# Dense 128x128 blocks for the split operands of the products with adj, and a state shuttle in runs of 32

## The chip, the cores and the metric

The kernel runs on one core of one Trainium2 chip. The metric is device time in microseconds (us) from one launch. Time before: 1607.32 us, the median of three runs (1606.89 to 1607.37).

## The reference, cut to what matters

Thirty-two graphs of 512 nodes with 128 features share one 512x512 matrix `adj`. Four layers follow one another, each a residual around a layer norm and a ReLU. Layer 1 is the one that the change touches: a gated graph network of five steps, whose state `h` is multiplied by `adj` in each of them.

```
h = relu(layernorm(x)); x = x + gcn(h, normalized adj)        # layer 0
h = relu(layernorm(x))                                        # layer 1
for five steps:
    m  = adj @ h
    z  = sigmoid([m, m] @ w3.T + h @ u3.T + b)
    r  = sigmoid([m, m] @ w4.T + h @ u3.T + b)
    hv = tanh([m, m] @ w5.T + (r * h) @ u5.T + b)
    h  = (1 - z) * h + z * hv
x = x + h
h = relu(layernorm(x)); x = x + elu(graph attention(h))       # layer 2
h = relu(layernorm(x)); x = x + graph attention(h)            # layer 3
```

So layer 1 has 32 x 5 = 160 products with `adj`, each of 512x512 by 512x128. Layer 0 has one product for each graph with the normalized matrix (named `an` in the program).

## The kernel before

**Tiles.** A graph's tokens stand in a tile of 128 partitions x 4 chunks (C = 4) x 128 features. In the steps of layer 1 the new state is made with features on the partitions (`hT`), because the gates' products want it so. The next product with `adj` wants it with tokens on the partitions (`h`).

**A product in three (`in_three`, from L604).** A float32 operand is split in a part with its upper bits and a rest, each held in the type fp32r: `cut` (DVE, L613, a bitwise and), `upper` (ACT, L615, a copy of `cut`), `lower` (DVE, L616, `h` less `cut`) and `across` (DVE, L617, formed of `cut` and `h`). `adj` is split in the same way once, at the start (`factors_of`, L417 to L432). TensorE then does twelve products of 128x128 weights with 512 columns (L623): four with `upper`, four with `lower`, then ACT scales the PSUM bank (L630), four with `across`, and ACT copies the bank to `m` (L632). The blocks of `upper`, `lower` and `across` are the weights, which TensorE loads ahead of each product (PEld); the split `adj` is what moves.

**The shuttle (L580 to L589).** In most steps the state is turned from features to tokens not by TensorE but by a DVE transpose of 32x32 blocks into `sq` (L584), four DMAs of 64 KB to DRAM (`far`) and one DMA of 256 KB back into `h`. Its argument `inner` says how `sq` is laid out inside a row of 128 elements: `"(c j)"` leaves runs of 32 elements, `"(j c)"` interleaves the four chunks, so that one chunk's elements lie 16 bytes apart. The shuttle of the steps passes `"(j c)"`. Such an `h` is marked `turned`, and `rows` then picks chunk c of the weights out of it with a step of four elements:

```python
def rows(t, c):
    return t.rearrange("p k (j c) -> p c (k j)", c=C)[:, c] if turned else t[:, c, :]
```

After the last step the same layout is read by the residual (L766). The first state of a graph, the layer norm's `y` of the attention layers (which keeps `"(c j)"`) and the first products of a graph are not `turned`. `shuttle_first` (L591) brings the first state the other way.

**The order.** `Plan` writes the order of all engines' instructions out when the program is built. Each piece of work is given to `op(engine, cost, due, emit, r, w, delay)`: its cost in us, a due time, what it reads and what it writes. A list scheduler plays the engines through with those costs, takes buffers from named pools (`"cut"`: 2, `"upper"`: 2, `"lower"`: 2, `"across"`: 3, `"sq"`: 2, eight PSUM banks), and issues the pieces in the order that comes out. The costs are thus no times of the chip; they set the order alone. `MR` is the cost of one product of L623, `V` that of a float32 DVE operation of 128x512, `A` that of an ACT operation of that size. On the chip each engine runs its own list in order and waits on semaphores. From a model time of 1342 on, the scheduler also fills gaps of TensorE with transposes into a free bank (L321).

**Gates and the rest.** `step` has five products of 128x128 by 128x512 in plain float32 (L729, L730, L736, L743, L744; two instructions each), the tanh operations (L732, L738, L746), and the DVE operations L734, L748, L749, L751. `gat` has the attention: L818, the DVE scores L859 and the mix L885 (L871 for the last four graphs).

Of the kernel before, what the change touches and what calls it, by code (L numbers as in the profile page):

```python
# [10 lines left out]
F32 = mybir.dt.float32  # L11
# [4 lines left out]
ALU = mybir.AluOpType  # L16
# [253 lines left out]
def gnn_stack(ctx: ExitStack, tc: tile.TileContext, a: dict, out: bass.AP):  # L270
# [50 lines left out]
        IDLE_FROM, lambda v: nc.tensor.transpose(v.t[:, 0, :], ident.t, ident.t))  # L321
    op = plan.op
    MM, MM1, TURN, MR = 0.858, 0.224, 0.111, 0.216
    V, A = 0.61, 0.585

    def fixed(shape, name, parts=1, dtype=F32):
        v = Val(None, parts)
# [67 lines left out]
    for c in range(C):  # L395
        p = Val("bank")
        turned.append(p)

        def turn_adj(c=c, p=p):
            for m in range(C):  # L400
                nc.tensor.transpose(p.t[:, m, :], adj_sb.t[:, c, m * P:(m + 1) * P], ident.t)
        op("PE", C * TURN, -800, turn_adj, r=[adj_sb[c], ident], w=[p])
        op("ACT", A, -800, lambda c=c, p=p: nc.scalar.copy(adjT.t[:, :, c * P:(c + 1) * P], p.t), r=[p], w=[adjT[c]])
        if c % 2 == 0:
            junk = Val("r")
            op("ACT", 0.7, -801, lambda c=c, junk=junk: nc.scalar.activation(
                flat(junk.t), adj_sb.t[:, c, :], AF.Copy, accum_out=deg.t[:, c:c + 1]), r=[adj_sb[c]], w=[junk, deg[c]])
# [9 lines left out]
    def factors_of(mT, name, due):  # L417


        upper, lower, across = [fixed([P, C, N], name + k, C, dtype=F32R) for k in ("1", "2", "3")]  # L420
        for c in range(C):
            cut = Val("cut")
            op("DVE", 0.35, due, lambda c=c, cut=cut: nc.vector.tensor_scalar(
                flat(cut.t).bitcast(I32), mT.t[:, c, :].bitcast(I32), UPPER, None, op0=ALU.bitwise_and), r=[mT], w=[cut])
            op("ACT", A, due, lambda c=c, cut=cut: nc.scalar.copy(upper.t[:, c, :], flat(cut.t)), r=[cut], w=[upper[c]])
            op("DVE", V, due, lambda c=c, cut=cut: nc.vector.tensor_sub(
                lower.t[:, c, :], mT.t[:, c, :], flat(cut.t)), r=[mT, cut], w=[lower[c]])
            op("ACT", A, due, lambda c=c: nc.scalar.mul(
                lower.t[:, c, :], lower.t[:, c, :].bitcast(F32), SPLIT), w=[lower[c]])
            op("DVE", V, due, lambda c=c, cut=cut: nc.vector.tensor_sub(  # L430
                across.t[:, c, :], lower.t[:, c, :].bitcast(F32), flat(cut.t)), r=[lower[c], cut], w=[across[c]])
        return upper, lower, across  # L432
    of_adj = factors_of(adjT, "adj", -3.6)

# [61 lines left out]
    def norm_stats(b, due):  # L496
        xb, st, mv, ve = xs[b], Val("st", C), Val("mv"), Val("ve")
        for c in range(C):
            op("DVE", 0.21, due, lambda c=c: nc.vector.bn_stats(st.t[:, c, :], xb.t[:, c, :]), r=[xb[c]], w=[st[c]])

        def aggr():
            for c in range(C):
                nc.vector.bn_aggr(mv.t[:, c, :], st.t[:, c, :])
            nc.vector.tensor_scalar_add(ve.t, mv.t[:, :, 1], EPS)  # L504
        op("DVE", 0.45, due, aggr, r=[st], w=[mv, ve])
        return mv, ve

    def norm_relu(b, y, due, times=None):
# [68 lines left out]
        op("PE", C * TURN, due, turns, r=[y, ident], w=[p, *then])  # L577
        return p

    def shuttle(src, squares, dst, due, soon, inner="(c j)"):  # L580


        sq, far = Val("sq"), Val("far", Q)
        op("DVE", 0.61, soon, lambda: nc.vector.transpose(  # L584
            sq.t.rearrange(f"p q {inner} -> p q c j", c=C), flat(src.t).rearrange(squares, c=C, q=Q)), r=[src], w=[sq])
        for k in range(Q):
            op("SP", 0.44, due, lambda k=k: nc.sync.dma_start(
                far.t[:, :, k, :].rearrange("q i f -> i q f"), sq.t[k * W:(k + 1) * W]), r=[sq], w=[far[k]], delay=4)
        op("SP", 0.4, due, lambda: nc.sync.dma_start(dst.t, far.t.rearrange("q i k f -> (q i) k f")), r=[far], w=[dst], delay=5)  # L589

    def shuttle_first(h, hT, due, soon):  # L591

        sq, far = Val("sq"), Val("far", Q)
        op("DVE", 0.61, soon, lambda: nc.vector.transpose(
            sq.t.rearrange("p k (c i) -> p k c i", c=C), h.t.rearrange("p c (k j) -> p k c j", k=Q)), r=[h], w=[sq])
        for q in range(Q):
            op("SP", 0.44, due, lambda q=q: nc.sync.dma_start(
                far.t[:, :, q, :].rearrange("k j f -> j k f"), sq.t[q * W:(q + 1) * W]), r=[sq], w=[far[q]], delay=4)
        for q in range(Q):
            op("SP", 0.4, due, lambda q=q: nc.sync.dma_start(  # L600
                hT.t.rearrange("p c (q i) -> q p c i", q=Q)[q], far.t.rearrange("k j q (c i) -> q (k j) c i", c=C)[q]),
               r=[far[q]], w=[hT[q]], delay=5)

    def in_three(h, turned, factors, due):  # L604

        cut, upper, lower, across = Val("cut"), Val("upper"), Val("lower"), Val("across")
        upper_of, lower_of, across_of = factors

        def rows(t, c):
            return t.rearrange("p k (j c) -> p c (k j)", c=C)[:, c] if turned else t[:, c, :]
        op("DVE", 0.35, due - 5, lambda: nc.vector.tensor_scalar(  # L613
            flat(cut.t).bitcast(I32), flat(h.t).bitcast(I32), UPPER, None, op0=ALU.bitwise_and), r=[h], w=[cut])
        op("ACT", A, due - 5, lambda: nc.scalar.copy(flat(upper.t), flat(cut.t)), r=[cut], w=[upper])  # L615
        op("DVE", V, due - 5, lambda: nc.vector.tensor_sub(flat(lower.t), flat(h.t), flat(cut.t)), r=[h, cut], w=[lower])  # L616
        op("DVE", V, due - 5, lambda: nc.vector.scalar_tensor_tensor(  # L617
            flat(across.t), flat(cut.t), 1 + 1 / SPLIT, flat(h.t), op0=ALU.mult, op1=ALU.subtract), r=[h, cut], w=[across])
        p, m = Val("bank"), Val("m")

        def times(left, right, first):
            for c in range(C):
                nc.tensor.matmul(flat(p.t), rows(left.t, c), right.t[:, c, :], start=first and c == 0, stop=c == C - 1,  # L623
                                 skip_group_check=True)

        def first_two():
            times(upper, upper_of, True)
            times(lower, lower_of, False)
        op("PE", 8 * MR, due, first_two, r=[upper, lower, upper_of, lower_of], w=[p])
        op("ACT", A, due - 6, lambda: nc.scalar.mul(flat(p.t), flat(p.t), 1 + 1 / SPLIT), w=[p])  # L630
        op("PE", 4 * MR, due, lambda: times(across, across_of, False), r=[across, across_of], w=[p, m])
        op("ACT", A, due - 6, lambda: nc.scalar.copy(flat(m.t), flat(p.t)), r=[p], w=[m])  # L632
        return m

    def product(h, due):

        p, m = Val("bank"), Val("m")
        for c in range(C):
# [5 lines left out]
                        nc.tensor.matmul(flat(p.t)[:, lo * P:hi * P], h.t[:, c, :], right, start=c == lo == 0,  # L644
                                         stop=c == C - 1, skip_group_check=True)
            op("PE", MM, due, times, r=[h[c], adjT, diag[c]], w=[p, m])
        op("ACT", A, due, lambda: nc.scalar.copy(flat(m.t), flat(p.t)), r=[p], w=[m])
        return m

    def normalized(begun):  # L650
# [56 lines left out]
    def ggnn(b, due):  # L707
# [4 lines left out]
        if FAR0 <= b < B - FAR1:  # L712
            shuttle_first(h, hT, due - 2.5, due - 3)
        else:
            p = to_features(h, due - 2, hT)
            op("ACT", A, due - 2, lambda hT=hT: nc.scalar.copy(flat(hT.t), flat(p.t)), r=[p], w=[hT])
        turned = False
        for s in range(STEPS):
            now = due + LANES * s
# [5 lines left out]
    def step(b, s, m, hT, due, lane):  # L725
# [30 lines left out]
        if not EARLY <= due < STEPS * B:  # L756
            p = to_features(new, due + 2, *([] if last else [h]))
            if last:
                op("DVE", V, due + 2, lambda: nc.vector.tensor_add(flat(xs[b].t), flat(xs[b].t), flat(p.t)),
                   r=[p, lane], w=[xs[b]])  # L760
            else:
                op("ACT", A, due + 1, lambda: nc.scalar.copy(flat(h.t), flat(p.t)), r=[p], w=[h])
            return h, False, new
        shuttle(new, "p (c q i) -> p q c i", h, due, due - 5, "(j c)")
        if last:
            op("DVE", V, due + 2, lambda: nc.vector.tensor_add(  # L766
                xs[b].t.rearrange("p c (k j) -> p k c j", k=Q), xs[b].t.rearrange("p c (k j) -> p k c j", k=Q),
                h.t.rearrange("p k (j c) -> p k c j", c=C)), r=[h, lane], w=[xs[b]])
        return h, True, new


# [25 lines left out]
    def gat(b, l, due):  # L797
# [4 lines left out]
        if near:  # L802
            rstd, g = center_relu(b, y, due), Val("off", 2)
            pT = to_features(y, due + 1, gT)
            op("ACT", A, due + 1, lambda: nc.scalar.copy(flat(gT.t), flat(pT.t)), r=[pT], w=[gT])
        else:
            norm_relu(b, y, due)
            shuttle(y, "p (c q j) -> p q c j", gT, due + 0.5, due)
# [47 lines left out]
            op("SP", 0.4, due + 1.5, lambda: nc.sync.dma_start(  # L856
                row.t, line.t.rearrange("c q i -> (c q i)").unsqueeze(0).to_broadcast([P, N])), r=[line], w=[row, e], delay=7)
        for j in range(C):
            op("DVE", 0.68, due + 3, lambda j=j: nc.vector.scalar_tensor_tensor(  # L859
                e.t[:, j, :], matrix(row), h.t[:, j, D + 1:D + 2], mask.t[:, j, :], op0=ALU.max, op1=ALU.mult),  # L860
               r=[row, h[2 + j // 2], mask], w=[e[j]])

# [112 lines left out]
```

## Time and profile before

| | |
|---|---|
| median of three runs | 1607.32 us |
| the profiled execution's own time | 1608.62 us |
| its span, first to last instruction | 1606.8 us |
| TensorE products (PE) | 1589.5 us busy, 6966 instructions |
| TensorE weight loads (PEld) | 1160.8 us busy |
| DVE | 1481.0 us busy, 3751 instructions |
| ACT | 905.6 us busy |
| POOL | 152.5 us busy |
| DMA | 157.66 MB, mean 98 GB/s |
| granted TensorE clock | 1.0 |

An engine's busy time is the union of its records, so records that overlap count once. A record of a product or of a DVE operation is longer than the step from one start to the next, since neighbours overlap. "By shape" below is the table of groups of instructions kept apart by operand shapes: line, engine, operation, output and input names, shapes and count, then busy us, mean ns of one, idle us of the engine just before them. The chain is the work that ended last, followed back from the end; in order of time its rows have a start, a length in us, the line and a count.

### The profile page before, as it was taken

What the parts mean: (1) busy time and instruction counts of PE and PEld (TensorE: products, weight loads), DVE (VectorE), ACT (ScalarE), POOL (GpSimd) and SP (SyncE); (2) the same over time, 40 slices, a digit from 0 to 9 for tenths busy, and PEclk for the clock granted to TensorE, in tenths of its full rate; (3) what the DMA queues carried; (4) which work ended last, traced back from release to release, by engine and by line L of the source; (5) the groups of instructions that cost most, each with busy time, mean ns of one, the idle gap of its engine ahead of it and who ended that gap; (6) DMA issues with size and microseconds to landing.
All of it is one profiled execution on the core that took longest, in us unless ns stands there. A gap on an engine that the chain in (4) does not pass through costs nothing.

```text
span 1606.8 us, 23090 instructions
## 1 busy us (share of the span) xinstructions
PE 1589.5 (99%) x6966; PEld 1160.8 (72%) x6966; DVE 1481.0 (92%) x3751; ACT 905.6 (56%) x1822; POOL 152.5 (9%) x137
## 2 busy tenths in 40 slices
PE   8899999999999999999999999999999999999998
PEld 7576667776777776777777686777676766767678
DVE  8989789999999999999999999999999899987888
ACT  6765555555555545645555645655655555555464
POOL 2111000000100101010110110101010000000010
PEclk9999999999999999999999999999999999999999
DMA  3134233444543443444433534444344424432201
GB/s 105 33 86 110 64 95 97 116 115 113 126 103 101 105 119 92 109 114 120 117 100 93 125 102 122 109 102 112 87 124 116 110 71 106 115 100 66 53 27 41
DMA packets 270141, 157.66 MB, mean 98 GB/s; under 512 B 81248, under 2 KB 236224, under 8 KB 270016
## 3 DMA queue, kind: packets, MB, share of 16 engines
q1 hardware_dynamic: 269728, 155.66, 38.0%
q8 instruction: 55, 0.90, 0.2%
q14 instruction: 70, 0.57, 0.1%
q10 hardware_dynamic: 288, 0.52, 0.1%
HBM read 86.25 MB, written 69.84 MB: 97 GB/s over the span
## 4 chain that ended last, share of the span: by engine, by line
PE 90%; DVE 7%; ACT 1%; issue 1%; POOL 0%; DMA 0%; DVEq 0%; ACTq 0%; POOLq 0%
PE bank L623 32%; PE bank L885 11%; PE bank L729 8%; PE bank L730 8%; PE bank L743 8%; PE bank L744 8%; PE bank L736 8%; PE bank L818 3%; PE bank L693 2%; PE bank L871 1%; DVE sq L584 1%; DVE e L859 1%; PE bank L576 0%; DVE hT L751 0%; DVE hv L748 0%
## 5 line engine op out<-in xcount | busy, mean ns | idle before, releaser
L512 POOL TENSOR_TENSOR rstd<-ve,mhalf 128x4 f32<-128x4 f32 x119 | 140.8, 1184 | 1366.1 <-DVE ve L504 1161.8
L885 PEld LDWEIGHTS bank<-h_gat,e 128*128 128x128 f32 x1792 | 210.5, 191 | 17.9 <-issue 14.4
L623 PE MATMUL bank<-adj,across 128*128 128x512 f32 x640 | 215.3, 462 | 1.6 <-ACT bank L630 1.6
L630 ACT ACTIVATE bank<-bank 128x512 f32<-128x512 f32 x188 | 109.3, 581 | 186.2 <-PE bank L623 183.6
L885 PE MATMUL bank<-h_gat,e 128*128 128x129 f32 x1792 | 212.2, 275 | 0.3 <-DVE v L890 0.3
L623 PE MATMUL bank<-adj,upper 128*128 128x512 f32 x640 | 201.2, 436 | 1.3 <-ACT upper L615 1.3
L623 PEld LDWEIGHTS bank<-adj,across 128*128 128x128 f32 x640 | 156.2, 280 | 41.6 <-issue 22.4
L732 ACT ACTIVATE r<-bank,gate_bw 128x512 f32<-128x512 f32 x160 | 109.7, 686 | 127.3 <-PE bank L730 118.4
L623 PE MATMUL bank<-adj,lower 128*128 128x512 f32 x640 | 177.0, 398 | 0.0
L623 PEld LDWEIGHTS bank<-adj,upper 128*128 128x128 f32 x640 | 154.4, 280 | 30.1 <-issue 8.8
L729 PE MATMUL bank<-m,wT 128*128 128x512 f32 x320 | 164.4, 595 | 3.0 <-ACT m L632 2.5
L736 PE MATMUL bank<-m,wT 128*128 128x512 f32 x320 | 163.4, 594 | 1.8 <-ACT r L732 1.8
L743 PE MATMUL bank<-m,wT 128*128 128x512 f32 x320 | 163.8, 593 | 0.7 <-DVE h_gat L836 0.6
L744 PE MATMUL bank<-rh,wT 128*128 128x512 f32 x320 | 163.5, 592 | 0.7 <-DVE rh L734 0.7
L584 DVE STREAM_TRANSPOSE sq<-hT 128x512 f32<-128x512 f32 x148 | 163.6, 1105 | 0.2
L730 PE MATMUL bank<-hT,wT 128*128 128x512 f32 x320 | 163.4, 592 | 0.0
L746 ACT ACTIVATE hv<-bank,gate_bw 128x512 f32<-128x512 f32 x160 | 109.5, 684 | 93.9 <-PE bank L744 93.0
L623 PEld LDWEIGHTS bank<-adj,lower 128*128 128x128 f32 x640 | 152.9, 280 | 7.2
L859 DVE SCALAR_TENSOR_TENSOR e<-row,h_gat,maskT 128x512 f32<-128x512 f32 x224 | 156.4, 740 | 0.0
L748 DVE TENSOR_TENSOR hv<-hv,hT 128x512 f32<-128x512 f32 x160 | 109.6, 686 | 42.4 <-ACT hv L746 41.9
L615 ACT CAST upper<-cut 128x512 fp32r<-128x512 f32 x188 | 115.2, 613 | 45.7 <-DVE cut L613 44.3
L632 ACT COPY m<-bank 128x512 f32<-128x512 f32 x188 | 109.9, 586 | 53.8 <-PE bank L623 53.3
(155 smaller groups left out, 2504.5 us busy)
## 6 DMA issues: line engine op xcount, KB each, us to landing
far<-sq SPq DMA_DIRECT2D x928, 64.0 KB
h<-far SPq DMA_DIRECT2D x148, 256.0 KB
gT<-far SPq DMA_DIRECT2D x56, 256.0 KB
row<-line SPq DMA_DIRECT2D x56, 256.0 KB
hT<-far SPq DMA_DIRECT2D x112, 64.0 KB
x<-in_x_dram SPq DMA_DIRECT2D x24, 256.0 KB
out_dram<-x SPq DMA_DIRECT2D x20, 256.0 KB
adjT<-in_x_dram SPq DMA_DIRECT2D x8, 256.0 KB
```

Of the source, the lines that this page charges most:

```text
L512: op("POOL", 1.0, due, lambda: nc.gpsimd.tensor_tensor(rstd.t, ve.t, mhalf.t, ALU.pow), r=[ve, mhalf], w=[rstd])
L584: op("DVE", 0.61, soon, lambda: nc.vector.transpose(sq.t.rearrange(f"p q {inner} -> p q c j", c=C), flat(src.t).rearrange(squares, c=C, q= ...
L615: op("ACT", A, due - 5, lambda: nc.scalar.copy(flat(upper.t), flat(cut.t)), r=[cut], w=[upper])
L623: nc.tensor.matmul(flat(p.t), rows(left.t, c), right.t[:, c, :], start=first and c == 0, stop=c == C - 1, skip_group_check=True)
L632: op("ACT", A, due - 6, lambda: nc.scalar.copy(flat(m.t), flat(p.t)), r=[p], w=[m])
L729: nc.tensor.matmul(flat(gate.t), gates.t[:, 0, :], flat(m.t), start=True, stop=False)
L730: nc.tensor.matmul(flat(gate.t), gates.t[:, 1, :], flat(hT.t), start=False, stop=True)
L736: op("PE", MM, due + 0.3, lambda: nc.tensor.matmul(flat(gate.t), gates.t[:, 2, :], flat(m.t), start=False, stop=True, skip_group_check=Tru ...
L743: nc.tensor.matmul(flat(cand.t), gates.t[:, 3, :], flat(m.t), start=True, stop=False)
L744: nc.tensor.matmul(flat(cand.t), u5T.t[:, 0, :], flat(rh.t), start=False, stop=True)
L859: op("DVE", 0.68, due + 3, lambda j=j: nc.vector.scalar_tensor_tensor(e.t[:, j, :], matrix(row), h.t[:, j, D + 1:D + 2], mask.t[:, j, :], ...
L885: nc.tensor.matmul(pt()[:, c, :D + 1], e.t[:, j, i * P:(i + 1) * P], h.t[:, j, :D + 1], start=(j == 0), stop=(j == C - 1))
```

## The change

The shuttle of the steps goes back to `"(c j)"`, the only layout left. `in_three` no longer picks weights with a step of four elements. Instead, where the state comes from a shuttle, `upper` (ACT) and `lower` (DVE) read it in a permuted order in runs of 32 elements and write four dense blocks. `across` is now made of `lower` and `upper` in place of `cut` and `h`, dense on both sides, and so waits for both. In `factors_of` the order of the third factor and the scaling is swapped, and the factor SPLIT sits on the other operand. The rest is costs handed to the scheduler: `V` 0.61 to 0.595, `A` 0.585 to 0.575, a new `COPY` of 0.495 for plain ACT copies and scalings, and smaller values at `cut`, `bn_stats`, the aggregate, the transposes and L859. The same instructions are issued, and no DMA changes in number, size or runs.

```diff
-    V, A = 0.61, 0.585
+    V, A, COPY = 0.595, 0.575, 0.495
...
-            op("ACT", A, due, lambda c=c: nc.scalar.mul(
+            op("DVE", V, due, lambda c=c, cut=cut: nc.vector.scalar_tensor_tensor(
+                across.t[:, c, :], flat(cut.t), -1 / SPLIT, lower.t[:, c, :].bitcast(F32), op0=ALU.mult, op1=ALU.add),
+               r=[lower[c], cut], w=[across[c]])
+            op("ACT", COPY, due, lambda c=c: nc.scalar.mul(
                 lower.t[:, c, :], lower.t[:, c, :].bitcast(F32), SPLIT), w=[lower[c]])
-            op("DVE", V, due, lambda c=c, cut=cut: nc.vector.tensor_sub(
-                across.t[:, c, :], lower.t[:, c, :].bitcast(F32), flat(cut.t)), r=[lower[c], cut], w=[across[c]])
...
-    def shuttle(src, squares, dst, due, soon, inner="(c j)"):
+    def shuttle(src, squares, dst, due, soon):
...
-        op("DVE", 0.61, soon, lambda: nc.vector.transpose(
-            sq.t.rearrange(f"p q {inner} -> p q c j", c=C), flat(src.t).rearrange(squares, c=C, q=Q)), r=[src], w=[sq])
+        op("DVE", 0.617, soon, lambda: nc.vector.transpose(
+            sq.t.rearrange("p q (c j) -> p q c j", c=C), flat(src.t).rearrange(squares, c=C, q=Q)), r=[src], w=[sq])
...
-        def rows(t, c):
-            return t.rearrange("p k (j c) -> p c (k j)", c=C)[:, c] if turned else t[:, c, :]
-        op("DVE", 0.35, due - 5, lambda: nc.vector.tensor_scalar(
+        if turned:
+            def given(t):
+                return t.rearrange("p k (c j) -> p c k j", c=C)
+
+            def made(t):
+                return t.rearrange("p c (k j) -> p c k j", k=Q)
+        else:
+            given = made = flat
+        op("DVE", 0.325, due - 5, lambda: nc.vector.tensor_scalar(
             flat(cut.t).bitcast(I32), flat(h.t).bitcast(I32), UPPER, None, op0=ALU.bitwise_and), r=[h], w=[cut])
-        op("ACT", A, due - 5, lambda: nc.scalar.copy(flat(upper.t), flat(cut.t)), r=[cut], w=[upper])
-        op("DVE", V, due - 5, lambda: nc.vector.tensor_sub(flat(lower.t), flat(h.t), flat(cut.t)), r=[h, cut], w=[lower])
+        op("ACT", COPY, due - 5, lambda: nc.scalar.copy(made(upper.t), given(cut.t)), r=[cut], w=[upper])
+        op("DVE", V, due - 5, lambda: nc.vector.tensor_sub(made(lower.t), given(h.t), given(cut.t)), r=[h, cut], w=[lower])
         op("DVE", V, due - 5, lambda: nc.vector.scalar_tensor_tensor(
-            flat(across.t), flat(cut.t), 1 + 1 / SPLIT, flat(h.t), op0=ALU.mult, op1=ALU.subtract), r=[h, cut], w=[across])
+            flat(across.t), flat(lower.t).bitcast(F32), -SPLIT, flat(upper.t).bitcast(F32), op0=ALU.mult, op1=ALU.add),
+           r=[lower, upper], w=[across])
...
-                nc.tensor.matmul(flat(p.t), rows(left.t, c), right.t[:, c, :], start=first and c == 0, stop=c == C - 1,
+                nc.tensor.matmul(flat(p.t), left.t[:, c, :], right.t[:, c, :], start=first and c == 0, stop=c == C - 1,
...
-        shuttle(new, "p (c q i) -> p q c i", h, due, due - 5, "(j c)")
+        shuttle(new, "p (c q i) -> p q c i", h, due, due - 5)
...
-                h.t.rearrange("p k (j c) -> p k c j", c=C)), r=[h, lane], w=[xs[b]])
+                h.t.rearrange("p k (c j) -> p k c j", c=C)), r=[h, lane], w=[xs[b]])
```

More of the change, by code (lines that the diff above doesn't have):

```diff
@@ L402, in gnn_stack @@
         op("PE", C * TURN, -800, turn_adj, r=[adj_sb[c], ident], w=[p])
-        op("ACT", A, -800, lambda c=c, p=p: nc.scalar.copy(adjT.t[:, :, c * P:(c + 1) * P], p.t), r=[p], w=[adjT[c]])
+        op("ACT", COPY, -800, lambda c=c, p=p: nc.scalar.copy(adjT.t[:, :, c * P:(c + 1) * P], p.t), r=[p], w=[adjT[c]])
         if c % 2 == 0:
@@ L422, in factors_of @@
             cut = Val("cut")
-            op("DVE", 0.35, due, lambda c=c, cut=cut: nc.vector.tensor_scalar(
+            op("DVE", 0.325, due, lambda c=c, cut=cut: nc.vector.tensor_scalar(
                 flat(cut.t).bitcast(I32), mT.t[:, c, :].bitcast(I32), UPPER, None, op0=ALU.bitwise_and), r=[mT], w=[cut])
-            op("ACT", A, due, lambda c=c, cut=cut: nc.scalar.copy(upper.t[:, c, :], flat(cut.t)), r=[cut], w=[upper[c]])
+            op("ACT", COPY, due, lambda c=c, cut=cut: nc.scalar.copy(upper.t[:, c, :], flat(cut.t)), r=[cut], w=[upper[c]])
             op("DVE", V, due, lambda c=c, cut=cut: nc.vector.tensor_sub(
                 lower.t[:, c, :], mT.t[:, c, :], flat(cut.t)), r=[mT, cut], w=[lower[c]])
-            op("ACT", A, due, lambda c=c: nc.scalar.mul(
+            op("DVE", V, due, lambda c=c, cut=cut: nc.vector.scalar_tensor_tensor(
+                across.t[:, c, :], flat(cut.t), -1 / SPLIT, lower.t[:, c, :].bitcast(F32), op0=ALU.mult, op1=ALU.add),
+               r=[lower[c], cut], w=[across[c]])
+            op("ACT", COPY, due, lambda c=c: nc.scalar.mul(
                 lower.t[:, c, :], lower.t[:, c, :].bitcast(F32), SPLIT), w=[lower[c]])
-            op("DVE", V, due, lambda c=c, cut=cut: nc.vector.tensor_sub(
-                across.t[:, c, :], lower.t[:, c, :].bitcast(F32), flat(cut.t)), r=[lower[c], cut], w=[across[c]])
         return upper, lower, across
@@ L498, in norm_stats @@
         for c in range(C):
-            op("DVE", 0.21, due, lambda c=c: nc.vector.bn_stats(st.t[:, c, :], xb.t[:, c, :]), r=[xb[c]], w=[st[c]])
+            op("DVE", 0.192, due, lambda c=c: nc.vector.bn_stats(st.t[:, c, :], xb.t[:, c, :]), r=[xb[c]], w=[st[c]])
         def aggr():
@@ L504, in aggr @@
             nc.vector.tensor_scalar_add(ve.t, mv.t[:, :, 1], EPS)
-        op("DVE", 0.45, due, aggr, r=[st], w=[mv, ve])
+        op("DVE", 0.33, due, aggr, r=[st], w=[mv, ve])
         return mv, ve
@@ L593, in shuttle_first @@
         sq, far = Val("sq"), Val("far", Q)
-        op("DVE", 0.61, soon, lambda: nc.vector.transpose(
+        op("DVE", 0.617, soon, lambda: nc.vector.transpose(
             sq.t.rearrange("p k (c i) -> p k c i", c=C), h.t.rearrange("p c (k j) -> p k c j", k=Q)), r=[h], w=[sq])
@@ L629, in in_three @@
         op("PE", 8 * MR, due, first_two, r=[upper, lower, upper_of, lower_of], w=[p])
-        op("ACT", A, due - 6, lambda: nc.scalar.mul(flat(p.t), flat(p.t), 1 + 1 / SPLIT), w=[p])
+        op("ACT", COPY, due - 6, lambda: nc.scalar.mul(flat(p.t), flat(p.t), 1 + 1 / SPLIT), w=[p])
         op("PE", 4 * MR, due, lambda: times(across, across_of, False), r=[across, across_of], w=[p, m])
-        op("ACT", A, due - 6, lambda: nc.scalar.copy(flat(m.t), flat(p.t)), r=[p], w=[m])
+        op("ACT", COPY, due - 6, lambda: nc.scalar.copy(flat(m.t), flat(p.t)), r=[p], w=[m])
         return m
@@ L646, in product @@
             op("PE", MM, due, times, r=[h[c], adjT, diag[c]], w=[p, m])
-        op("ACT", A, due, lambda: nc.scalar.copy(flat(m.t), flat(p.t)), r=[p], w=[m])
+        op("ACT", COPY, due, lambda: nc.scalar.copy(flat(m.t), flat(p.t)), r=[p], w=[m])
         return m
@@ L715, in ggnn @@
             p = to_features(h, due - 2, hT)
-            op("ACT", A, due - 2, lambda hT=hT: nc.scalar.copy(flat(hT.t), flat(p.t)), r=[p], w=[hT])
+            op("ACT", COPY, due - 2, lambda hT=hT: nc.scalar.copy(flat(hT.t), flat(p.t)), r=[p], w=[hT])
         turned = False
@@ L761, in step @@
             else:
-                op("ACT", A, due + 1, lambda: nc.scalar.copy(flat(h.t), flat(p.t)), r=[p], w=[h])
+                op("ACT", COPY, due + 1, lambda: nc.scalar.copy(flat(h.t), flat(p.t)), r=[p], w=[h])
             return h, False, new
-        shuttle(new, "p (c q i) -> p q c i", h, due, due - 5, "(j c)")
+        shuttle(new, "p (c q i) -> p q c i", h, due, due - 5)
         if last:
@@ L804, in gat @@
             pT = to_features(y, due + 1, gT)
-            op("ACT", A, due + 1, lambda: nc.scalar.copy(flat(gT.t), flat(pT.t)), r=[pT], w=[gT])
+            op("ACT", COPY, due + 1, lambda: nc.scalar.copy(flat(gT.t), flat(pT.t)), r=[pT], w=[gT])
         else:
@@ L858, in gat @@
         for j in range(C):
-            op("DVE", 0.68, due + 3, lambda j=j: nc.vector.scalar_tensor_tensor(
+            op("DVE", 0.65, due + 3, lambda j=j: nc.vector.scalar_tensor_tensor(
                 e.t[:, j, :], matrix(row), h.t[:, j, D + 1:D + 2], mask.t[:, j, :], op0=ALU.max, op1=ALU.mult),
```

## The prediction

> **What bounds the kernel now.** First the page's busy times, then the same by stretches of 100 us.
>
> ```profile
> PE 1589.5 (99%) x6966; PEld 1160.8 (72%) x6966; DVE 1481.0 (92%) x3751; ACT 905.6 (56%) x1822; POOL 152.5 (9%) x137
> ```
>
> ```profile
> 0.00:100.00 100.00, 91.04 (x396) 64.96 (x397) 87.67 (x302) 71.62 (x148) 19.47 (x24) 1.00 0.28 69
> ...
> 900.00:1000.00 100.00, 100.00 (x438) 73.04 (x437) 96.51 (x239) 55.53 (x114) 9.24 (x8) 1.00 0.45 115
> ```
>
> The columns of the second fence are PE, PEld, DVE, ACT and POOL busy. TensorE never rests between 100 and 1500 us: the stretches there lack 3.2 us together, the first 100 us lack 9.0 (chains of latency while the first graphs start), and the end about 5. DVE is second at 92%, and up to 96.5% in mid-run. So time can go in two ways only: TensorE's own steps get shorter, or the few waits around them go. A full PE says nothing on what a product costs, since records overlap; the step from one end to the next does. That is read from the chain of waits in order of time, whose rows here are L623 back to back, and from the weight loads' own line.
>
> ```profile
> L623 PEld LDWEIGHTS bank<-adj,lower x640: 187/310/313, 33.6 to 1541.4; 128*128 128x128 f32 x160
> L623 PEld LDWEIGHTS bank<-an,lower x112: 187/188/191, 62.9 to 1246.9; 128*128 128x128 f32 x112
> ```
>
> ```profile
> 76.96 7.47 PE bank L623 x32
> ```
>
> ```profile
> 174.65 2.84 PE bank L623 x12
> ```
>
> ```profile
> 807.19 1.90 PE bank L623 x8
> ...
> 811.66 0.89 PE bank L693 x8
> 812.56 2.02 PE bank L623 x8
> ```
>
> The first two rows give shortest/median/longest ns of a weight load. There are two kinds and nothing between: about 188 ns (dense: all of `an`, and `adj` where the state is not `turned`) and about 310 ns (the step of four). The trace has 1440 of the latter, 120 products of twelve. Yet a load of 310 ns does not make a product of 310 ns: the 32 products at 76.96 us, all dense, take 7.47/32 = 233 ns each, the twelve strided ones at 174.65 us 2.84/12 = 237 ns. The third fence shows where the stride does bite: eight strided products behind a long float32 product (L730) take 1.90 us, but behind L693, whose products last 0.89/8 = 0.11 us, 2.02 us. A load of 310 ns doesn't fit beside 110 ns of work, so 0.12 us stick out, once per such place.
>
> Last, DVE by shape:
>
> ```profile
> L584 DVE STREAM_TRANSPOSE sq<-hT 128x512 f32<-128x512 f32 x148 | 163.6, 1105 | 0.2
> L584 DVE STREAM_TRANSPOSE sq<-y 128x512 f32<-128x512 f32 x56 | 39.4, 704 | 5.7 <-ACT y L518 5.6
> L594 DVE STREAM_TRANSPOSE sq<-h 128x512 f32<-128x512 f32 x28 | 19.7, 703 | 0.0
> L766 DVE TENSOR_TENSOR x<-x,h 128x512 f32<-128x512 f32 x20 | 21.8, 1091 | 0.0
> ```
>
> The same transpose takes 1105 ns where it writes with a step of 16 bytes (`hT`) and 704 ns in runs of 32 (`y`, `h`); the addition L766, which reads `h` in that step, takes 1091 ns where other additions of the size take some 685 ns.
>
> **What the Trainium skill says.** "SBUF — State Buffer", Specifications (TRN2): lines of 16 bytes, at least two hits in a line for full bandwidth. A step of four fp32 hits each line once. The trace agrees for DVE (+401 ns on the transpose, +406 on the addition) and for the weight load (+122 ns), and runs of 32 show no penalty. "TensorE: Matmul & The Clock Gate", Step-by-step: the next weights load while the present product streams; the trace agrees, 310 ns of load inside a step of 237. "Perfetto Trace Analysis", Identifying the Most-Contended Engine: matmul busy time is a poor measure, weight-load busy a better one. Here the 72% of weight loads would promise much; the steps on the chain say 4 ns, and I go by those. The first-named TensorE page, Architectural detail: ACT and DVE take instructions strictly in order. That matters for the new wait below.
>
> **The change part by part.**
>
> *Weights dense (TensorE, on the path).* (a) 1440 products at 237 instead of 233 to 234 ns: 3.7 ns each, 5.3 us. (b) Groups that follow a short product: the trace has 35 strided groups behind L693 (12), L818 (16) and L885 (7), 0.12 us each: 4.2 us. (c) 107 groups behind L730 or L744 start about 10 ns later than dense ones: 1 us. Sum 10.5 us, all of it steps of an engine without rest. Nothing hides it, and no other engine has to follow faster than it can (next part).
>
> *Transposes and residual (DVE, beside TensorE).* 148 transposes by 0.40 us are 59 us, 28 additions at L766 by 0.41 are 11 us: DVE falls from 1481 to about 1411 us. Worth directly nothing, because TensorE runs over it. Its use is slack: waits of TensorE in mid-run that DVE causes (L836, L890, L895, or ACT behind DVE) can shrink. They are part of the 3.2 us; I take 2 us.
>
> *`upper` and `lower` read permuted.* No row shows ACT or DVE reading a subtraction or a copy in exactly this way. From below: no gain is possible, as the element counts are the same, so +0. From above: the 16-byte step's +0.41 us, on 120 of `lower` (49 us on DVE) and 120 of `upper` (49 us on ACT, which has 1606.8 - 905.6 = 701 us free). I take +0, because the transposes L584 (`y`) and L594 read runs of 32 and cost 704 ns, 20 above a flat operation. Even at the upper end DVE stands at 1460 us, below today.
>
> *`across` from `lower` and `upper`.* The operation stays one DVE operation of 684 ns with two SBUF inputs. New is that it waits for ACT's L615. Behind it on DVE, in order, stand the other lanes' L734, L748 to L751, L859 and the norms; ACT and then TensorE wait for these. From below: 0, where the order puts it after `upper`. From above: if the order stayed as it is, the starts of L617 and ends of L615, paired in order, have `upper` late in 23 of 188 cases, by 39 us together. I take 10 us of DVE time and 0 of TensorE, covered by the 70 us just freed. `across` itself is needed only after eight products and L630. `cut` and `h` come free one operation earlier, `upper` no later, since L623 still reads it last.
>
> *`factors_of`.* One 0.6 us DVE operation goes ahead of ACT's scaling for each of eight blocks. For `adj` the last scaling ends at 26.0 us and the first L623 starts at 32.8; for `an` the last operation ends at 45.6 and the first use is at 62.1. Zero, hidden by these 7 and 16 us.
>
> *The order.* The costs change, so every engine's list is dealt anew. The new ones lie nearer to what this trace shows from start to start: L630 494 ns against `COPY` 0.495, L859 656 against 0.65, `bn_stats` 193 against 0.192, while 0.61 for the `hT` transpose was far from its 0.94 to 1.0 us. That speaks for no more waits than now; bounds -3 and +12 us, taken as part of the 2 us above.
>
> *DMA.* Four stores of 64 KB and a load of 256 KB per shuttle, unchanged in runs of 128 elements; they start up to 0.4 us sooner on SP's queue, at a DMA share of 38%. Zero.
>
> Sum on the profiled execution: 1606.8 - 10.5 - 2 = 1594.3 us of span; its own time lies 1.8 above (1608.62 - 1606.8): 1596.1. The median of the runs lies 1.3 below that execution: 1594.8, so 1595.
>
> **The rivals.**
>
> *More than that (0.07).* The freed DVE also ends the waits at the start and the tail. For: 70 us of slack. Against: the first 100 us wait on chains through ACT, and the tail has no shuttles. All of mid-run and half of the rest: 1606.8 - 10.5 - 3 - 7, about 1587.
>
> *Given back by the order (0.11).* Same mechanism, but the re-dealt lists cost 6 us or so of new waits: 1600 to 1604. For: TensorE has lists of 6966 products with no slack anywhere.
>
> *The loads were never in the way (0.07).* The 4 ns and the 0.12 us are other traffic, or the dense loads keep their wait: 1604 to 1609. Against: the two kinds of groups stand side by side in the same stretches.
>
> *Slower: DVE blocked behind ACT (0.05).* Each L617 parks DVE until L615 is done. DVE has 123 us idle now and 70 more after, so 193 us over 188 products: from a mean wait of 1.0 us on, DVE is the bound. To lose 3 us against now it must also eat TensorE's gain of 12, another 15 us: 1.1 us. At 1.2 us DVE needs 1411 + 226 - the waits that fall in its idle time (at most some 10): 1627 us. Against: 39 us in all even in the old order.
>
> **How the numbers follow.** My case has 0.70. The range 1587 to 1604 takes in the gain of all waits and the order giving back most; some 13 in 100 lie above and 5 below. 0.2% (3.2 us) is about what a measurement of this kernel can tell from no change. Faster by more: my case, the first rival and nearly all of the second, 0.87. Within: 0.07. Slower: 0.06.
>
> **What would show it.** Weight loads of L623 all near 188 ns with PEld busy down by 1440 x 0.122 = 176 us, to about 985; L584 from `hT` near 704 and L766 near 685; DVE busy 1400 to 1425; twelve L623 in 2.80 us; `lower` at 683 to 700; PE still at 99%. Wrong would be: L617 with idle time before it ended by L615 in the tens of us and PE below 98%; `lower` near 1090; or no drop in the steps of L623.

## The result, and the profile after

The changed kernel takes 1588.34 us (median of four runs, 1587.70 to 1589.26) against 1607.34: a ratio of 0.9881, with a 95% interval of 0.9864 to 0.9898. That is 19.0 us saved, where 12 were forecast. The profiled execution has a span of 1586.1 us (1606.8 before) and a time of 1587.88.

First the page's busy times of the kernel after, then the stretch from 900 to 1000 us (columns: PE, PEld, DVE, ACT and POOL busy):

```profile
PE 1573.8 (99%) x6966; PEld 1077.6 (68%) x6966; DVE 1424.2 (90%) x3751; ACT 902.6 (57%) x1822; POOL 153.0 (10%) x137
```

```profile
900.00:1000.00 100.00, 100.00 (x440) 68.39 (x439) 94.11 (x264) 58.16 (x116) 12.59 (x11) 1.00 0.42 106
```

TensorE is as full as it was, and DVE has lost 57 us. The weight loads and the DVE operations by line and by shape (the product of three is now L631, the transpose L585, the residual L774):

```profile
L631 PEld LDWEIGHTS bank<-adj,lower x640: 187/188/189, 32.8 to 1524.8; 128*128 128x128 f32 x160
```

```profile
L624 DVE SCALAR_TENSOR_TENSOR across<-lower,upper 128x512 fp32r<-128x512 f32 x188 | 127.1, 678 | 3.9 <-PE bank L631 2.4 <-ACT upper L622 0.6
...
L623 DVE TENSOR_TENSOR lower<-h,cut 128x512 fp32r<-128x512 f32 x160 | 108.3, 678 | 3.2 <-PE bank L631 2.1
L585 DVE STREAM_TRANSPOSE sq<-hT 128x512 f32<-128x512 f32 x148 | 103.4, 699 | 0.2
...
L774 DVE TENSOR_TENSOR x<-x,h 128x512 f32<-128x512 f32 x20 | 13.5, 675 | 0.0
```

Every load of L631 now takes 186 to 192 ns; the second kind is gone. The transpose fell from 1105 to 699 ns, the residual from 1091 to 675. `lower`, read in runs of 32, costs 678 ns, no more than the flat one did, and ACT's `upper` stayed at 613. The new wait is in the last column of L624: DVE stood idle 0.6 us in all for ACT's `upper`. There is a second new wait, which the prediction did not have: since `across` now reads `upper`, the profile has ACT idle 10.4 us ahead of `upper` (14 times) until an L624 was done. ACT's idle time ahead of `upper` still fell from 45.7 to 33.1 us in all.

The chain of waits in order of time (start us, length us, line, count; L826 is the L818 of before):

```profile
783.27 0.89 PE bank L826 x8
784.16 0.93 PE bank L631 x4
...
789.38 2.79 PE bank L631 x12
```

Twelve products take 2.79 us, 233 ns each, and four of them right behind L826's short products take 0.93 us: nothing sticks out any more.

**Where the 20.7 us of span went.** Records of TensorE overlap (a product of L631 has a record of 395 ns and a step of 233), so a wait shorter than the overlap of some 160 ns leaves no gap. I therefore took each product's step, from the end of the one before to its own end, less 233 ns for the product of three, 429 for half a gate product, 112 for the 128-wide ones. What was over is summed in us: in the column "stride" what strided products took more than dense ones, and by stretch of time all the rest:

| profiled execution | stride | first 60 us | middle | last 150 us |
|---|---|---|---|---|
| before | 10.0 | 14.2 | 8.3 | 3.7 |
| after | 0 | 9.7 | 1.5 | 4.2 |

So 10.0 us are the strided loads, 4.5 lie in the start, 6.8 in the middle, and the tail gives 0.5 back: 20.8. What shortened the start was not taken apart.

### The profile page after: what moved, and what is told of

Read it like the earlier page. It is cut to its first block, busy times and chain, and to the rows that moved or that the text cites. A ratio compares the mean times of both kernels' runs of the same rounds, so it can differ in the third digit from the quotient of the medians.

```text
span 1586.1 us, 23092 instructions
## 1 busy us (share of the span) xinstructions
PE 1573.8 (99%) x6966; PEld 1077.6 (68%) x6966; DVE 1424.2 (90%) x3751; ACT 902.6 (57%) x1822; POOL 153.0 (10%) x137
## 4 chain that ended last, share of the span: by engine, by line
PE 93%; DVE 5%; ACT 1%; issue 0%; POOL 0%; DMA 0%; DVEq 0%; POOLq 0%; ACTq 0%
PE bank L631 32%; PE bank L893 12%; PE bank L737 9%; PE bank L744 9%; PE bank L751 8%; PE bank L752 8%; PE bank L738 8%; PE bank L826 3%; PE bank L701 2%; DVE e L867 1%; PE bank L879 1%; DVE st L554 0%; DVE st L500 0%; PE bank L577 0%; POOL rstd L513 0%
## 5 line engine op out<-in xcount | busy, mean ns | idle before, releaser
L631 PE MATMUL bank<-adj,across 128*128 128x512 f32 x640 | 209.6, 453 | 0.0
L631 PE MATMUL bank<-adj,upper 128*128 128x512 f32 x640 | 200.4, 435 | 0.0
L631 PE MATMUL bank<-adj,lower 128*128 128x512 f32 x640 | 175.1, 395 | 0.0
L744 PE MATMUL bank<-m,wT 128*128 128x512 f32 x320 | 163.3, 594 | 1.8 <-ACT r L740 1.8
L631 PEld LDWEIGHTS bank<-adj,across 128*128 128x128 f32 x640 | 118.0, 189 | 59.6 <-issue 39.2
L631 PEld LDWEIGHTS bank<-adj,upper 128*128 128x128 f32 x640 | 118.8, 188 | 53.2 <-issue 22.6
L746 ACT ACTIVATE z<-bank,gate_bw 128x512 f32<-128x512 f32 x160 | 109.8, 686 | 73.5 <-PE bank L744 69.4
L631 PEld LDWEIGHTS bank<-adj,lower 128*128 128x128 f32 x640 | 120.2, 188 | 28.8
L622 ACT CAST upper<-cut 128x512 fp32r<-128x512 f32 x188 | 114.9, 613 | 33.1 <-DVE cut L620 17.8
```

The lines of the kernel that those rows point to most:

```text
L622: op("ACT", COPY, due - 5, lambda: nc.scalar.copy(made(upper.t), given(cut.t)), r=[cut], w=[upper])
L631: nc.tensor.matmul(flat(p.t), left.t[:, c, :], right.t[:, c, :], start=first and c == 0, stop=c == C - 1, skip_group_check=True)
L744: op("PE", MM, due + 0.3, lambda: nc.tensor.matmul(flat(gate.t), gates.t[:, 2, :], flat(m.t), start=False, stop=True, skip_group_check=Tru ...
L746: op("ACT", A, due - 5, lambda: nc.scalar.activation(flat(z.t), flat(gate.t), AF.Tanh, bias=gate_b["w3"].t, scale=0.5), r=[gate, gate_b["w ...
```

## The experiments

Two theories on what stands beside the strided loads. One: DVE's relief takes waits away from TensorE. Two: the new costs give a better order, whatever the layout. A third showed itself on the way: it also counts whether the lists were made with DVE's load in the costs. All times are medians; the kernel before ran beside them at 1607.0 to 1607.7 us.

| run | layout of the state and weights | costs | us | ratio to before, 95% |
|---|---|---|---|---|
| after | runs of 32, dense | new | 1588.3 | 0.9881 (0.9864 to 0.9898) |
| step of four alone | runs, weights strided | new | 1599.2 | 0.9949 (0.9936 to 0.9961) |
| more DVE work | runs, dense, DVE loaded | new | 1616.8 | 1.0055 (1.0042 to 1.0068) |
| old layout | as before | new | 1613.3 | 1.0037 (1.0024 to 1.0049) |
| old costs | runs, dense | old | 1593.2 | 0.9911 (0.9898 to 0.9925) |
| before, new costs | as before | new | 1621.2 | 1.0091 (1.0076 to 1.0105) |
| more DVE work, priced | runs, dense, DVE loaded | new, and that work | 1602.2 | 0.9966 (0.9953 to 0.9979) |
| before, priced | as before | new, and the slow DVE work | 1600.9 | 0.9966 (0.9953 to 0.9979) |

**The step of four alone.** Same lists in the same order as after.

```diff
+        given = made = flat
+        def rows(t, c):
+            return t.rearrange("p k (j c) -> p c (k j)", c=C)[:, c] if turned else t[:, c, :]
...
-                nc.tensor.matmul(flat(p.t), left.t[:, c, :], ...
+                nc.tensor.matmul(flat(p.t), rows(left.t, c), ...
```

> The changed kernel with the weights of the products with adj picked with a step of four elements again, while the shuttle keeps its runs of 32 and all DVE and ACT operations stay flat and quick; every engine has the same list in the same order as in the changed kernel. The weights picked so are those of other tokens, so this leaves the right pairing of tokens out. My theory (strided weight loads cost TensorE some 10.5 us in steps of L623 and behind short products): 1588.3 + 10.5 = about 1599 us, steps of twelve products back at 2.84 us. Rival (the loads were never in the way, all is order and DVE): 1588 to 1590 us.

Measured 1599.24 us, 10.9 above the changed kernel (give or take 3.4 from the two intervals). The loads and the chain of this run (L627 is the product of three, L822 the L826 of after):

```profile
L627 PEld LDWEIGHTS bank<-adj,lower x640: 187/310/313, 33.9 to 1536.0; 128*128 128x128 f32 x160
```

```profile
789.00 0.89 PE bank L822 x8
789.89 1.05 PE bank L627 x4
...
795.23 2.83 PE bank L627 x12
```

Loads of 310 ns are back, twelve products take 2.83 us, and four behind the short L822 1.05 instead of 0.93: the two terms of the prediction, side by side. The rival that the loads were never in the way is out.

**More DVE work.** Also after's order, with the weights dense.

```diff
+    def more_dve():
+        nc.vector.tensor_sub(idle_dve, idle_dve, idle_dve)   # 128x328
...
+            more_dve()      # ahead of each transpose of the state, and of each L774
```

> The changed kernel with one more DVE subtraction of 328 elements (about 0.40 us) ahead of each of the 148 transposes of the state and each of the 28 residual additions L774, in the same piece of work, so that DVE is loaded and late as before while the weights stay dense and the order of all lists stays. If the 8 us beyond the strided loads come from DVE's relief: 1593 to 1596 us, DVE busy near 1495. If they come from the new order: at most 1590 us. If TensorE's bound hides DVE wholly: 1588 us.

Measured 1616.76 us: 28.4 slower than after and slower than before, far beyond all three expectations. The dose was a little high: the added subtraction takes 0.41 us from start to start, 72 us for 176 of them, and DVE is busy 1488 us against 1481 in the kernel before. The stretch from 100 to 1450 us of this run, then of the kernels after and before:

```profile
100.00:1450.00 1350.00, 1335.83 (x5617) 886.31 (x5616) 1252.33 (x3201) 744.21 (x1455) 117.93 (x100) 1.00 0.41 106
```

```profile
100.00:1450.00 1350.00, 1349.93 (x5747) 908.30 (x5746) 1215.48 (x3093) 759.13 (x1486) 120.78 (x103) 1.00 0.42 107
```

```profile
100.00:1450.00 1350.00, 1346.83 (x5667) 974.94 (x5667) 1260.43 (x3077) 756.26 (x1479) 122.20 (x103) 1.00 0.42 106
```

PE is the first busy column, DVE the third. With DVE at 1252 us TensorE lacks 14.2 us; the kernel before had DVE at 1260, busier, and lacked 3.2. Counted by steps, the middle loses 28.9 us here and 8.3 before. So DVE's share alone doesn't set the loss. The chain's shares by engine, of this run and of the kernel after (they don't add up to 100; in the first, the chain accounts for some 75% of the span):

```profile
PE 37%; DVE 30%; issue 3%; ACT 2%; DMA 2%; POOL 1%; SPq 0%; DVEq 0%; POOLq 0%; ACTq 0%
```

```profile
PE 93%; DVE 5%; ACT 1%; issue 0%; POOL 0%; DMA 0%; DVEq 0%; POOLq 0%; ACTq 0%
```

DVE has come onto the path with 30%. One group of TensorE by shape of this run (a gate product) shows who was late there:

```profile
L761 PE MATMUL bank<-m,wT 128*128 128x512 f32 x320 | 164.8, 596 | 3.7 <-DVE h_gat L857 1.8 <-DVE v L911 1.2 <-DVE x L916 0.5
```

It isn't the operation that grew: these gate products wait for `h_gat` and `v` of the attention, which stand in DVE's list when it is behind. The row holds 3.7 us of TensorE's gaps; other groups have theirs for ACT, so this is an example and not the whole account.

**The old layout in after's order.**

```diff
-            sq.t.rearrange("p q (c j) -> p q c j", c=C), ...
+            sq.t.rearrange(f"p q {inner} -> p q c j", c=C), ...    # steps: "(j c)"
...
+        given = made = flat
...
-                nc.tensor.matmul(flat(p.t), left.t[:, c, :], ...
+                nc.tensor.matmul(flat(p.t), rows(left.t, c), ...
...
-                h.t.rearrange("p k (c j) -> p k c j", c=C)), ...
+                h.t.rearrange("p k (j c) -> p k c j", c=C)), ...       # the residual
```

> The layout of the kernel before, whole (shuttle in the step of 16 bytes, weights with the step of four, flat splits, L774 strided), in the changed kernel's order with its costs, and with across made of lower and upper. If the strided loads cost 10.5 us and the rest of the gain is DVE's relief: about 1605 to 1607 us, as before. If the rest is the order: about 1599 us, the same as with the step of four alone.

Measured 1613.27 us, outside both: 14.0 over the step of four alone, for the slow transposes and residual, 51 us of DVE's busy time. In steps, the middle lost 15.5 us and the stride 10.0. DVE's slowness costs more in this order than the 8.3 us that the middle of the kernel before lost to all waits.

**Old costs.**

```diff
-    V, A, COPY = 0.595, 0.575, 0.495
+    V, A, COPY = 0.61, 0.585, 0.585      # and 0.61, 0.35, 0.21, 0.45, 0.68 in their places
```

> The changed kernel with the costs of the kernel before handed to the scheduler (V 0.61, A and COPY 0.585, transposes 0.61, cut 0.35, bn_stats 0.21, aggregate 0.45, scores 0.68), so only the order differs. If the 8 us beyond the strided loads come from the order by the new costs: about 1596 us. If they come from DVE's relief: 1588 to 1591 us.

Measured 1593.2 us: between the two. The layout alone is worth 14.1 us in an order by the old costs (10.9 of it the stride), and the new costs 4.9 more.

**The new costs alone on the kernel before.**

> The kernel before, whole, with only the changed kernel's costs handed to the scheduler (transposes of the state at 0.617, though they take 1.0 us in this layout). If the gain beyond the strided loads is in the new order by itself: about 1602 us, 5 faster than before. If the new costs are good only with quick transposes, because they no longer overprice the rest of DVE and so leave some 110 us of its work unpriced: 1610 to 1615 us, slower than before, like the old layout in the changed kernel's order (1613.3).

Measured 1621.2 us, 14 slower than before, further than expected. The costs suggest why. Summed over all DVE pieces, the program before priced 1422.6 us, and DVE was busy 1481 on the chip: 58 unpriced. The changed program prices 1370.9 for 1424: 53. The old layout with the new costs has 1370.9 for 1477: 106. The old costs overpriced most DVE operations (`V` 0.61 against 0.60 from start to start, `bn_stats` 0.21 against 0.193, the aggregate 0.45 against some 0.34), and that made up, in sum, for transposes at 0.61 that take 0.94 from start to start.

**The same DVE work, priced.** Two runs put the slow work into the costs.

```diff
-        op("DVE", 0.617, soon, turn, ...
+        op("DVE", 1.02 if more else 0.617, soon, turn, ...
-            op("DVE", V, due + 2, residual, ...
+            op("DVE", 1.0, due + 2, residual, ...
```

> The same instructions as in the run with more DVE work (1616.8 us), with that work's 0.40 us added to the costs of the transposes and of the residual, so only the order differs. If DVE's load itself stops TensorE at this level: at least 1610 us. If it was that the order did not know of it: 1590 to 1596 us.

Measured 1602.15 us: half of the 28.4 us is gone, by the order, with all the DVE work still there (the lists differ besides in 16 of the transposes that fill TensorE's gaps near the end). 13.8 us stay, which neither expectation had. The stretch of this run:

```profile
100.00:1450.00 1350.00, 1341.96 (x5713) 901.58 (x5712) 1268.64 (x3246) 753.21 (x1472) 118.45 (x102) 1.00 0.42 107
```

TensorE still lacks 8.0 us.

The second is the kernel before with the new costs, and its own slow transposes at 1.02 and residual at 1.0:

> The kernel before with the new costs and its slow transposes and strided residual at what they take (1.02 and 1.0 us). If an order that knows DVE's load removes the waits: 1588.3 + 10.9 for the strided loads + 0 to 5 = 1599 to 1604 us. If DVE's load itself costs TensorE: 1607 us or more.

Measured 1600.93 us: 20.3 faster than the same work with the new costs and the slow operations unpriced, 6.4 faster than before. Its stretch:

```profile
100.00:1450.00 1350.00, 1347.62 (x5701) 980.21 (x5701) 1263.70 (x3079) 754.88 (x1472) 120.13 (x102) 1.00 0.41 106
```

DVE is nearly as busy as in the run just shown (1263.70), and TensorE lacks 2.4 us. Less the 10.9 of the stride this is 1590.0, within 2 us of the changed kernel, though DVE carries all its old work (its list has 20 of the filling transposes fewer, 0.11 us each).

So the two pairs agree that an order which knows DVE's load is worth 14.6 and 20.3 us, and disagree on what the load costs beyond that: 13.8 us in the first, 1.7 in the second. Two differences are known. DVE has more to do in the first, 1488.9 us against 1479.4. And the price of 1.02 is generous for a slow transpose, which takes 0.94 us from start to start, but not for the added subtraction with a quick one, 0.41 + 0.63 us. Which of them counts is not shown.

All runs of this question together, rounded: DVE's busy time less the sum of its costs, and what the middle lost by steps.

| run | unpriced, us | middle, us |
|---|---|---|
| after | 53 | 2 |
| old costs | 7 | 5 |
| before, priced | 38 | 6 |
| before | 58 | 8 |
| more DVE work, priced | 47 | 15 |
| old layout | 106 | 16 |
| before, new costs | 106 | 23 |
| more DVE work | 117 | 29 |

More than 100 us unpriced goes with 16 us lost or more, less than 60 with 15 or less. Within either half the sum doesn't set the order: it is a rough sign, and not the whole cause.

**How far a time hangs on the draw of the order.** Three neutral changes of one cost.

```diff
-    V, A, COPY = 0.595, 0.575, 0.495
+    V, A, COPY = 0.594, 0.575, 0.495      # and 0.597 in another run; before: V 0.612 for 0.61
```

> The changed kernel with V at 0.594 in place of 0.595: no better and no worse a price, but another order comes out. It measures how far a time hangs on the order alone. If orders with fair prices are alike: 1586 to 1591 us. If the changed kernel's order is a lucky draw: 1592 to 1597 us, which would make the gain of the new costs over the old ones (1593.2) none that can be told.

> The changed kernel with V at 0.597, another neutral draw. Fair prices alike: 1586 to 1591 us; a lucky draw before: 1592 to 1597 us.

> The kernel before with V at 0.612 in place of 0.61, a neutral draw of its order. If the old costs, by overpricing the rest of DVE, make up for the underpriced transposes: 1604 to 1611 us. If the kernel before had a lucky order among bad ones: 1612 to 1622 us, like the runs with 110 us of DVE work unpriced.

Measured 1588.54 and 1591.57 us (ratios 0.9879 and 0.9901): of three neutral draws the changed kernel's is the fastest, by 0.2 and 3.2 us, so it is not much of a lucky one, but 3 us are in the draw. The kernel before came to 1603.95 (ratio 0.9975, 0.9966 to 0.9984), just below what was expected, 3.8 us faster than the kernel before that ran beside it. Part of the gain of 19.0 us may thus be the draw that the kernel before happened to have: against this neighbour some 15 would be left, 4 to 5 beyond the strided loads.

**TensorE's price.** The product of three at 0.2335, as the trace has it, in place of 0.216.

> The changed kernel with the cost of a product of L631 at 0.2335 in place of 0.216, which is the step the trace shows (233 to 234 ns). If what still stands between the changed kernel and TensorE's own steps is an order that underprices TensorE: 1583 to 1587 us. If the remaining waits are the start and the tail: 1587 to 1590 us. The due times and the model time from which gaps are filled were set with the other price, so some us of loss are possible.

Measured 1593.05 us (0.9911, 0.9897 to 0.9925), 4.7 slower. A truer price is not a better order by itself. Why was not settled: the due times and the model time that go with the price were left, and the step is of the size of one draw.

**Without the new wait.**

```diff
-        op("DVE", V, due - 5, lambda: nc.vector.scalar_tensor_tensor(
-            flat(across.t), flat(lower.t).bitcast(F32), -SPLIT, flat(upper.t).bitcast(F32), op0=ALU.mult, op1=ALU.add),
+        op("DVE", V, due - 5, lambda: nc.vector.tensor_sub(
+            made(across.t), given(h.t), given(cut.t)),
```

> The changed kernel in the same order, with across written by a permuted subtraction of cut from h (lower over again), so that it doesn't wait for ACT's upper any more; this leaves the formula of across out. If the new wait of DVE for ACT is hidden: 1587 to 1589.5 us, as the changed kernel. If it costs TensorE: 1583 to 1586 us.

Measured 1605.42 us (0.9986), 17 slower, which says nothing on the wait: DVE now stood idle before L624 for another reason.

```profile
  DMA h<-far: 17.0, 11
```

The row is from L624's own view, us and times. The scheduler gives `h` away once `lower` is made; in the same order `across` then reads the buffer after the next load into it was issued, and DVE waits for that DMA eleven times. The experiment swapped one wait for a worse one. What the new wait costs is known from the kernel after alone, 0.6 us of idle DVE. In this one run, 17.0 us of blocked DVE stand beside 17.1 us more of time.

## Why the prediction was right, and where its sum was short

**Weights dense, 10.5 us: right.** The step of four alone measures 10.9, the steps in the trace 10.0. The two large terms are there: 237 against 233 ns, and 0.12 us behind short products. The third is smaller than I had it: behind L730 and L744 the first strided step is 2 ns longer than a dense one by the median, not 10. The Trainium skill's page "TensorE: Matmul & The Clock Gate" (Step-by-step: the next weights load while a product streams) and the steps on the chain led to 4 ns a product; the 122 ns of the load itself would have promised 176 us.

**Costs of zero: right for the permuted reads, `factors_of` and the wait.** `lower` and `upper` came out at the lower bound, and DVE idled 0.6 us for `upper`, not 10. That `upper` would come free no later was wrong: ACT waited 10.4 us for L624 to have read it, but ACT had that time to spare. The rival that DVE is blocked behind ACT is out; its sum began from 123 us of idle DVE, where the page gives 125.8, which changes nothing in it.

**Waits, 2 us: this term was mis-sized.** The runs put 8.1 us (19.0 - 10.9) there; the profiled pair shows 10.8, 4.5 of it in the first 60 us, which I had taken as fixed. The mistake was in the reading: I said myself that busy records overlap, and then took TensorE's gaps in mid-run, 3.2 us, as all that waits could cost. By steps it was 8.3, because a wait shorter than the overlap leaves no gap. So the measured time lies near the low end of the range, closer to the first rival (about 1587) than to my case of 1595. Of what that rival named, mid-run and the start did give time, and the tail did not.

**"Directly nothing" for DVE's relief: right in sign, wrong as an argument.** I argued that TensorE runs over DVE as long as DVE's busy time stays under today's 1481 us. The old layout in after's order has DVE at 1477 and pays 14 us; the priced kernel before has it at 1479 and, less the stride, comes within 2 us of the changed kernel. So busy time doesn't bound what DVE costs; whether the lists were dealt with its load in them was worth 14.6 and 20.3 us, though one priced run still paid 13.8. My bound for the permuted reads, "even at the upper end DVE stands below today", was no bound either. The old layout in after's order has 51 us more DVE work than the step of four alone and pays 14.0 us for it; by the same rate, which is an estimate, the 49 us feared there would have cost some 13, more than the whole gain forecast.

**DVE's fall, 70 us: 57 came.** I took the transpose's gain from its records, 1105 less 704 ns, and records of DVE overlap too. Where DVE has no gap, a transpose of the state takes 0.94 us from start to start before and 0.63 after, the residual 1.00 and 0.60: 148 x 0.32 + 28 x 0.40 = 58 us.

**The order, -3 to +12 us: the sign was right for this layout only, and that was luck.** I argued that the new costs lie nearer to the trace. The argument would have held for the kernel before as well, and there they made it 14 us slower. How the 8.1 us split is open: 3.2 by the layout and 4.9 by the costs along one path, but a draw moves either end by 3 to 4 us. The costs of ACT changed together with DVE's, and the two were not tried apart.

**What would show it.** Loads of 188 ns, twelve in 2.80 us and DVE's 1424 us came as written, and L585 (699 ns), L774 (675) and `lower` (678) within 10 ns. PEld busy did not: 1077.6, not 985. I had summed durations, but a 310 ns load overlaps its neighbours, and a union only counted the 237 ns of the step, so 1440 x (237 - 188) = 71 of the 83 us that went.

## What to carry to other kernels

Price a weight load by what it adds to the step of its products, and look for it behind short products, where there is nothing to hide it. Where an engine's order is written out ahead of time, a slower or faster operation must be told to whoever writes the order: the same work moved by 20 us in one pair of runs and 15 in another when its cost was known, and a share of 90% busy says little of whether an engine is on the path. Measure waits from end to end, and an operation's cost from start to start, not from gaps and lengths of records that overlap.

## What the runs showed of the hardware

A stationary operand picked with a step of 16 bytes loads in 310 ns instead of 188, yet a stream of 512-column fp32r products slows only from 233 to 237 ns. DVE pays for the same step whether it writes it (a transpose, 1105 against 699 ns by its record, 0.94 against 0.63 us from start to start) or reads it as one of two inputs (an addition, 1091 against 675 ns, 1.00 against 0.60 us), and neither DVE (678 ns) nor ACT (613) pays anything for runs of 32 elements.
